# Two step-order tables exchanged in a two-layer graph network on one core

## The chip, the cores and the metric

The kernel runs on one core of one Trainium2 chip. The metric is the device time of one launch in microseconds (us). The kernel before takes 2598.3 us, the median of three runs (2597.79 to 2598.43).

## What is computed

64 graphs of 256 nodes with 512 features, all with one adjacency matrix, pass through two layers. Each layer normalises its input, applies a ReLU, and adds its result to the input. Layer 0 multiplies with the adjacency and then with a weight. Layer 1 is attention with 8 heads of 64 features over the neighbours. Cut to what matters:

```python
h = jnp.maximum(_layernorm(x), 0.0)
x = x + (einsum('nm,bmd->bnd', adj, h) @ w0 + b0)          # layer 0
h = jnp.maximum(_layernorm(x), 0.0)
q, k, v = h @ Wq + bq, h @ Wk + bk, h @ Wv + bv             # layer 1, 8 heads of 64
scores = q @ k.T / 8 + (1 - adj) * -1e9
x = x + softmax(scores) @ v @ Wo + bo
```

All of it is in fp32; a matmul call is two instructions on PE (TensorE).

## The kernel before

**Groups and stages.** Two graphs (GB = 2) make a group of 512 rows; there are NG = 32 groups. Layer 0 runs over all groups first and leaves its results in DRAM (`residual`, `hidden`). Then a loop over g runs layer 1. One turn of it holds, in this order on PE:

- `attend(g, 0)`: the denominators (`pden`, L1248) and softmax times v (`pav`, L1255) for the first half of the heads (qd = 0) of both graphs of the group
- `score(g, 1)`: scores of the second half (`sc`, L1207); DVE (VectorE) adds the mask while it moves each one out of PSUM (L1214)
- **the QK stage**: q and k of group g + 1, in the order of the table `QK` (L1427)
- `attend(g, 1)` and `score(g + 1, 0)`
- **the VO stage**: v of group g + 1 and the output projection of group g, in the order of the table `VO` (L1457)

`QK` is used for g = 1 to 30, 30 times; `VO` for g = 2 to 29, 28 times. Earlier groups use a plainer form, and the last ones the tables `V1`, `O1` and `OL`.

**A projection as steps.** A 512 by 512 product is not done directly. `quartered` (from L589) splits it by Strassen's scheme in Winograd's form into seven half-size products, named A to G; most of these are split the same way once more. It makes a dictionary of small steps, each named by a letter for the matrix (q, k, v, o), a letter for the product, and a letter or digit for the part. `follow` (L836) carries them out in the order of the table: a token is one step, `|` ends a tick, and `x` issues one waiting exponent of the softmax on ACT (ScalarE). So a table fixes the order of instructions on PE, ACT and DVE, and through the ticks also when deferred work on POOL (GpSimd) is issued.

For a product F or G the steps a, c, d and f are matmuls into a small sum bank (`q_Fs`), b, e and g copy intermediate sums from it on ACT, h and l add on DVE, and i, j and k are matmuls into the main bank `pa`. For C, D and E the steps b, e, f and h copy or add the sums into the result in SBUF, and i, j, k and l handle the remaining part. In such a chain a matmul may not start before the copy or addition that reads the sum ahead of it. Steps p and m move a whole main bank into the result or add it there. What `part` and `place` of `quartered` give is a region of the result.

**The steps that the prediction follows.** E of v ends with three steps: `El0` is a copy on ACT, `El1` and `El2` are additions on DVE. They finish the part of v that belongs to the first half of the heads and the second graph:

```python
for name, i, k in (("El1", 0, 0), ("El2", 1, None)):        # L829
    def todo(i=i, k=k):
        o = part(place(0, 1), i, k)
        add(o, part(banks["pa"], i, k), o)
    step(name, todo, "pa")
```

`attend(g, 0)` of the next turn reads v by halves f of 32 columns, then by graph b, then by 128-row tile k, then by four heads, which lie beside each other in PE's columns:

```python
for f in range(2):                                           # L1250
    for b in range(GB):
        v = V[g][qd, b]
        for k in range(NT):
            for h in range(4):
                nc.tensor.matmul(po[f][...], v[:, k, h * HD + f * 32:...], A[h // 2, b][...], ...)
```

**PSUM banks.** There are eight banks. `bank` (L299) takes the first one of the list of free banks that fits, and `give` (L312) appends a bank at the end of the list when its last step has been issued. The list is worked out while the program is built; on the chip the first matmul into a bank waits until the last reader of its former content has finished. So the order of the steps also decides which step waits for which.

**Deferred work.** `after(n, ...)` puts work off by n ticks. On POOL these are the key sums (L1239), the sums of inputs to the smaller products (L516, L619) and part of the softmax's reciprocal (L1272 to L1274). The next h is summed after the last matmul of v has been issued (`multiplied`). SP issues the DMAs: outputs once both halves of a graph are added up, then the next h and the next residual.

Of the kernel before, what the change touches and what calls it, by code (L numbers as in the profile page):

```python
# [73 lines left out]
def general_path(tc, x, adj, w0, b0, wq, bq, wk, bk, wv, bv, wo, bo, out):  # L74
# [137 lines left out]


QK = (
    "qA0 kA0 qFa kA1 qFb x kA2 | qFc kFa qFd kFb kA3 qFe x qCa | qBa kFc kFd qFf kp000 qA1 qFg qA2 kFe | qFh "
    "kp001 qA3 kFf qp000 kCa qBb kFg kCb kFi qBc | kFj kFh qp001 kFk kCc x kFl qBd kCd kCi qCb kCj kCe qBn kCk | "
    "kCf kp100 qCc kCl qFi kp101 qFj qFk qBe x kCg qFl qDa qBf | kGi kCh qBg kGj qp100 kGk qBk qCd qp101 kBa qCe "
    "kBb qCf qBh | kBc qBi qDb kBn qBj qGi qp110 qGj kBd qp111 qGa kBe qGk | qGb qDc qDd qCg qDe qGc qDf qGd kBf "
    "qCh qGe qDi | kBg qDj qDk kBk qGf qm10 qDg qGg qEa kGa qDh qEb kBh | kBi qGh kGb kBj qGl kDa kp110 kGc kGd "
    "kDb kp111 kEa qm11 qEc kGe | qEd kEb kDc qEf kDd kGf qEe kDe kEc kDf kGg kEd qEi qEf2 | kEf kDi kGh kDg kEe "  # L220
    "kGl kDj kDk qEg km11 qEj qEk | qCi kEf2 qEl0 qCj kDh qCk km10 kEi kEj kEk qCl kEg kEl0 | qEh qEl1 kEl1 kEh "
    "qEl2 kEl2 ")
VO = (
    "vA0 oBz vA1 oAz vA2 vA3 x | vCi vFa vCj vCk vFb vBa vp00 vBb vFc x | vFd vCa vCl vFi vFj vFe vFk vCb vBc oA0 "
    "vBn | vFf vCc vFg vGa vCd vBd vFh oA1 x vFl oA2 | vBe vDa vCe vGb oA3 vCf vp10 vBf op00 vGc vBg vGd | vCg "
    "vDb vGe vGi vBk x vGj vCh vGf vDc vDd oFa vGg | vDe vGk vDf oFb vEa vBh vGh vEb vBi vGl vBj oEa vp11 vEc | "
    "oEb vEd oFc vEf vm11 oFd vEe vDi oFe vDg vEf2 vDj vDh vDk | vEi vm10 vEj vEk oGa vEl0 oFf oGb vEg vEl1 oFg "
    "oFi vEl2 | oEc vEh oGc oFj oFh oFk oEd oFl oGd oCa oGe oDa | op10 oB0 oB1 oDb oCb oGf oEe oB2 oEf oGg | oB3 "
    "oGh oGi op11 oGj oGk oCc oGl oCd | oDc oDd oCe oEg om11 oDi oDj oDk oCf oCi oDe | oCj oDf oCk oEi oEh oCg "
    "oCl0 oEj oEk oDg oCl1 | oEl om10 oCh oDh ")  # L230
V1 = (
    "vA0 vFa vA1 vFb vA2 x vFc | vFd vA3 vCa vFe vEa vp00 vGa vFf vEb | vB0 vGb vFg vCb vFi x vGc vFh vGd vFl vCc "
    "vCd vGe | vDa x vCe vB1 vCf vFj vFk vGf vp10 vCg vEc | vCh vEd vGg vB2 vDb x vGh vGi vGj vDc vGl vEf vDd | "
# [1281 lines left out]
```

## Time and profile before

| | |
|---|---|
| median of 3 runs | 2598.3 us |
| profiled execution | 2598.07 us, of which the span is 2596.3 us |
| a QK stage (matmul start to `pden`) | 22.53 us |
| a VO stage | 22.67 us |
| one turn of the loop, QK stage at 1219.50 to the next at 1280.92 | 61.42 us |
| granted PE clock | 1.00 |

In the profile's rows PE is the matmul, PEld the load of its weights, which overlaps it. A row of the timeline gives the start in us, the time from its first start to its last end, engine, source line, operation, tiles out<-in, shape and how many instructions follow one another. All additions of these stages carry the line L850, because a helper issues them; the tile names tell them apart. Matmuls are pipelined, so the row of two 128-wide instructions lasts 0.39 us while the next row begins 0.22 us later: starts have to be compared, not lengths.

### The profile page before, as it was taken

Reading aid. Unit: us, or ns where it says so; the run is one execution under the profiler, and the core shown is the slowest. Engines: PE = TensorE matmul, PEld = TensorE weight load, DVE = VectorE, ACT = ScalarE, POOL = GpSimd, SP = SyncE. Lnnn points to the kernel's source line nnn. Section 1 sums busy time; section 2 is a strip of 40 time slices with the busy share of each in tenths; the row PEclk is TensorE's granted clock in tenths of the full one; section 3 lists DMA queues with packets and bytes.
Section 4 is the critical chain, followed back from the end, with each engine's and each line's share of the span. In section 5 each row is a group of like instructions: output and inputs, shape, how many; then the busy total and the mean of one; then the engine's idle time right before and its main releaser. Section 6 shows DMA issues by size and latency. Waiting matters only on the chain.

```text
span 2596.3 us, 57453 instructions
## 1 busy us (share of the span) xinstructions
PE 2582.3 (99%) x22046; PEld 2306.2 (89%) x22046; DVE 1941.8 (75%) x4284; ACT 1266.9 (49%) x2930; POOL 1834.3 (71%) x2262
## 2 busy tenths in 40 slices
PE   9999999999999999999999999999999999999999
PEld 8999899988888888889888888888888888889887
DVE  6888888885467777777777777777777777777776
ACT  4544444443344545555554545555444545555553
POOL 6788887773687777776666666777777777776664
PEclk9999999999999999999999999999999999999999
DMA  5776666565111222111111111111111222211111
GB/s 148 194 196 182 169 167 181 162 158 135 33 50 50 65 63 63 57 50 50 50 50 50 50 50 50 50 50 50 50 50 51 66 62 62 56 50 50 50 34 51
DMA packets 281111, 211.40 MB, mean 81 GB/s; under 512 B 145920, under 2 KB 212992, under 8 KB 280832
## 3 DMA queue, kind: packets, MB, share of 16 engines
q1 hardware_dynamic: 280224, 206.89, 29.8%
q8 instruction: 176, 2.88, 0.5%
q10 hardware_dynamic: 608, 0.79, 0.1%
q14 instruction: 103, 0.84, 0.1%
HBM read 106.96 MB, written 100.66 MB: 80 GB/s over the span
## 4 chain that ended last, share of the span: by engine, by line
PE 92%; POOL 3%; DVE 2%; ACT 1%; DMA 1%; issue 1%; SPq 0%; DVEq 0%; POOLq 0%; ACTq 0%
PE sc L1207 9%; PE pav L1255 8%; PE pden L1248 2%; PE q_pa L671 2%; PE k_pa L671 2%; PE v_pa L671 2%; PE o_pa L671 2%; PE q_pa L685 2%; PE v_pa L685 2%; PE o_pc L685 2%; PE o_pa L685 2%; PE k_pa L685 2%; PE q_pc L671 2%; PE k_pc L671 2%; PE v_pc L671 1%; PE q_Ds L671 1%
## 5 line engine op out<-in xcount | busy, mean ns | idle before, releaser
L1214 DVE SCALAR_TENSOR_TENSOR a<-sc,maskT 128x512 f32<-128x512 f32 x512 | 312.1, 682 | 237.4 <-PE sc L1207 237.4
L1272 POOL TENSOR_TENSOR as<-as 128x512 f32<-128x512 f32 x64 | 80.7, 1260 | 415.3 <-ACT as L1271 409.1
L1239 POOL TENSOR_TENSOR as<-a 128x512 f32<-128x512 f32 x256 | 318.4, 1274 | 32.9 <-ACT a L1232 27.5
L1232 ACT ACTIVATE a<-a 128x1024 f32<-128x1024 f32 x256 | 271.8, 1062 | 3.6 <-DVE a L1214 3.6
L1255 PE MATMUL pav<-a,v 128*32 128x256 f32 x4096 | 232.7, 379 | 0.0
L1255 PEld LDWEIGHTS pav<-a,v 128*32 128x32 f32 x4096 | 132.9, 110 | 88.1
L43 DVE BATCH_NORM_STATS2 st<-x 128x6 f32<-128x512 f32 x256 | 173.2, 676 | 8.7 <-DMA x<-in_x_dram 6.5
L1262 ACT ACTIVATE as<-pden 128x512 f32<-128x512 f32 x64 | 38.4, 600 | 226.7 <-PE pden L1248 226.7
L1031 ACT ACTIVATE h<-x,nb,rs 128x512 f32<-128x512 f32 x128 | 97.2, 807 | 96.4 <-POOL nb L55 93.9
L1207 PE MATMUL sc<-qk 64*128 64x256 f32 x1024 | 119.2, 382 | 0.0
L1207 PE MATMUL sc<-q,k 64*128 64x256 f32 x1024 | 119.2, 382 | 0.0
L1207 PEld LDWEIGHTS sc<-q,k 64*128 64x128 f32 x1024 | 97.1, 187 | 22.4 <-issue 13.2
L1207 PEld LDWEIGHTS sc<-qk 64*128 64x128 f32 x1024 | 97.1, 187 | 22.3 <-issue 13.1
L708 ACT COPY q_F<-q_Fs 128x128 f32<-128x128 f32 (+1 forms) x90 | 27.1, 301 | 183.2 <-PE q_Fs L671 183.2
L902 ACT ACTIVATE h<-x,nb,rs 128x512 f32<-128x512 f32 x124 | 90.8, 803 | 51.0 <-POOL nb L55 46.6
L965 POOL TENSOR_TENSOR hs<-h 128x512 f32<-128x512 f32 x31 | 39.4, 1271 | 72.9 <-ACT h L902 72.9
L1037 DVE STREAM_TRANSPOSE r<-h 128x512 f32<-128x512 f32 x128 | 84.0, 689 | 6.8 <-ACT h L1031 4.2
L619 POOL TENSOR_TENSOR spare<-h1T,spare 128x128 f32<-128x128 f32 x180 | 82.3, 457 | 7.0
L850 DVE TENSOR_TENSOR x<-o_pa,x 128x512 f32<-128x512 f32 (+1 forms) x121 | 82.8, 685 | 4.5 <-PE o_pa L685 3.1
L516 POOL TENSOR_TENSOR t_y<-yT,t_y 128x512 f32<-128x512 f32 (+1 forms) x65 | 82.7, 1272 | 3.2 <-ACT yT L937 0.8
L1274 POOL TENSOR_TENSOR as<-as 128x512 f32<-128x512 f32 x64 | 80.6, 1259 | 5.4
L309 ACT ACTIVATE o_pc<-bo_r 128x512 f32<-128x512 f32 x30 | 18.0, 601 | 134.6 <-DVE a L1214 134.6
(1659 smaller groups left out, 8882.5 us busy)
## 6 DMA issues: line engine op xcount, KB each, us to landing
residual<-x SPq DMA_DIRECT2D x256, 128.0 KB, 2.6
hidden<-r SPq DMA_DIRECT2D x128, 256.0 KB, 4.4
h1T<-hidden SPq DMA_DIRECT2D x64, 512.0 KB, 7.1
x<-residual SPq DMA_DIRECT2D x32, 1024.0 KB, 8.1
x<-in_x_dram SPq DMA_DIRECT2D x254, 128.0 KB, 3.0
out_dram<-x SPq DMA_DIRECT2D x62, 512.0 KB, 3.6
w_sb<-in_L_gnn_weight_dram SPq DMA_DIRECT2D x1, 1024.0 KB, 9.7
wq_sb<-in_L_gnn_Wq_dram SPq DMA_DIRECT2D x1, 1024.0 KB, 7.2
```

Of the source, the lines that this page charges most:

```text
L43: nc.vector.bn_stats(st, src)
L671: nc.tensor.matmul(o[:, 0, :], lhs, rhs, start=bool(fresh), stop=True, skip_group_check=True)
L685: nc.tensor.matmul(t[:, m, :], lhs, rhs, start=starts, stop=True, skip_group_check=True)
L850: nc.vector.tensor_tensor(o, ps, u, op=ALU.add)
L902: nc.scalar.activation(H0[g][:, t, :], xt[:, t, :], AF.Relu, bias=nb[:, t % n:t % n + 1], scale=rs[:, t % n:t % n + 1])
L1031: nc.scalar.activation(h1[:, k * NT + t, :], xt[:, k * NT + t, :], AF.Relu, bias=nb[:, t:t + 1], scale=rs[:, t:t + 1])
L1037: nc.vector.transpose(r[:, :, k, t, :], h1[:, k * NT + t, :].rearrange("p (j b) -> p j b", b=32))
L1207: nc.tensor.matmul(ps[j][:, kt * N:(kt + 1) * N], k[j * HD:(j + 1) * HD, c, kt * P:(kt + 1) * P], q[j * HD:(j + 1) * HD, c, :], start=(kt ...
L1214: nc.vector.scalar_tensor_tensor(o.rearrange("p k n -> p (k n)"), ps[j], SCALE, maskT_f, op0=ALU.mult, op1=ALU.add)
L1232: nc.scalar.activation(a, a, AF.Exp)
L1239: nc.gpsimd.tensor_tensor(AS[c, b], a4[:, :, 0, :], a4[:, :, 1, :], op=ALU.add)
L1255: nc.tensor.matmul(po[f][h * 32:(h + 1) * 32, b * N:(b + 1) * N], v[:, k, h * HD + f * 32:h * HD + f * 32 + 32], A[h // 2, b][:, (h % 2) * ...
```

## The change

Two constants change: the strings `QK` and `VO`. Each new string holds the same tokens as the old one (190 and 176 with the ticks and the exponents), in another order; steps, shapes and instructions stay as they are. The other tables are the same.

```diff
 QK = (
-    "qA0 kA0 qFa kA1 qFb x kA2 | qFc kFa qFd kFb kA3 qFe x qCa | qBa kFc kFd qFf kp000 qA1 qFg qA2 kFe | qFh "
-    "kp001 qA3 kFf qp000 kCa qBb kFg kCb kFi qBc | kFj kFh qp001 kFk kCc x kFl qBd kCd kCi qCb kCj kCe qBn kCk | "
-    "kCf kp100 qCc kCl qFi kp101 qFj qFk qBe x kCg qFl qDa qBf | kGi kCh qBg kGj qp100 kGk qBk qCd qp101 kBa qCe "
-    "kBb qCf qBh | kBc qBi qDb kBn qBj qGi qp110 qGj kBd qp111 qGa kBe qGk | qGb qDc qDd qCg qDe qGc qDf qGd kBf "
-    "qCh qGe qDi | kBg qDj qDk kBk qGf qm10 qDg qGg qEa kGa qDh qEb kBh | kBi qGh kGb kBj qGl kDa kp110 kGc kGd "
-    "kDb kp111 kEa qm11 qEc kGe | qEd kEb kDc qEf kDd kGf qEe kDe kEc kDf kGg kEd qEi qEf2 | kEf kDi kGh kDg kEe "
-    "kGl kDj kDk qEg km11 qEj qEk | qCi kEf2 qEl0 qCj kDh qCk km10 kEi kEj kEk qCl kEg kEl0 | qEh qEl1 kEl1 kEh "
-    "qEl2 kEl2 ")
+    "kFa kA0 kFb kA1 kFc qFa x qCa | kFd kBa kA2 qFb kA3 kFe x qA0 | kFf qFc qFd kFg qA1 kp000 kFh qA2 kp001 | "
+    "qA3 qFe kFl qBa qp000 qBb qFf qp001 kBb | kFi qFg kFj qCb qBc qFi qFh qBn kFk kBc qCc qFl x qCd kBd qCe kCa "
+    "| qCf qBd kBn qFj kCb kp100 qFk qBe qCg kp101 kBe kCc qCh qp100 kCd qBf | qp101 kCe kBf kCf qDa qBg kGi kBg "
+    "qDb kGj x qBk kGk kBk kCg qGi | kCh qGj qGk qDc qDd qCi qDe qGa qDf qCj | qGb kGa qCk kGb qGc qCl qDg qGd "
+    "kGc qDh qGe kGd | kDa kGe qGf kDb qEa qGg kBh kBi qEb kBj qGh qBh qGl | kp110 qBi qEc kp111 qEd qBj qEe kEa "
+    "kGf qp110 qEf2 kDc | qp111 kDd kDi kEb kDe kDj kDf kGg kDk qDi qEf qm11 qDj qDk | kEc kGh kEd kGl qEi kEe "
+    "qEj qEk kEf km11 kDg qEl0 qEg | kEf2 kCi kDh kCj kCk qEh kEi qEl1 kEj qEl2 kEk kEg kCl kEl0 | qm10 kEh km10 "
+    "kEl1 kEl2 ")
 VO = (
-    "vA0 oBz vA1 oAz vA2 vA3 x | vCi vFa vCj vCk vFb vBa vp00 vBb vFc x | vFd vCa vCl vFi vFj vFe vFk vCb vBc oA0 "
-    "vBn | vFf vCc vFg vGa vCd vBd vFh oA1 x vFl oA2 | vBe vDa vCe vGb oA3 vCf vp10 vBf op00 vGc vBg vGd | vCg "
-    "vDb vGe vGi vBk x vGj vCh vGf vDc vDd oFa vGg | vDe vGk vDf oFb vEa vBh vGh vEb vBi vGl vBj oEa vp11 vEc | "
-    "oEb vEd oFc vEf vm11 oFd vEe vDi oFe vDg vEf2 vDj vDh vDk | vEi vm10 vEj vEk oGa vEl0 oFf oGb vEg vEl1 oFg "
-    "oFi vEl2 | oEc vEh oGc oFj oFh oFk oEd oFl oGd oCa oGe oDa | op10 oB0 oB1 oDb oCb oGf oEe oB2 oEf oGg | oB3 "
-    "oGh oGi op11 oGj oGk oCc oGl oCd | oDc oDd oCe oEg om11 oDi oDj oDk oCf oCi oDe | oCj oDf oCk oEi oEh oCg "
-    "oCl0 oEj oEk oDg oCl1 | oEl om10 oCh oDh ")
+    "vA0 oAz vA1 oBz vA2 vA3 x | vCi vFa vCj vCk vFb vBa vp00 vBb vFc x | vDa vFd vCl vFi vFj vFe vFk vBc oA0 vBn "
+    "| vFf vCa vFg oA1 vCb oA2 vFh x vFl oA3 | vGa op00 vBd vp10 vCc vCd vBe oB0 vGb vDb vCe oFi | vCf vGi vGj x "
+    "vBf vDc vDd vGc vDe vBg vGd | vDf oFj vGe vGk vBk vCg vDg vCh vGf oFa vDh vGg vBh | vEa oFb vBi vGh vEb vBj "
+    "vGl oFc vp11 oFd vEc vEd oFe | vm11 oCa vEe vDi vEf vDj oCb oFf vEf2 vDk oFg oGa vm10 vEi oGb vEj | vEk oFh "
+    "vEg vEl0 oFk oGc vEh oGd oEa oFl oGe oCc | oCd oEb oGf op10 oDa oGg oEc oEd oDb oB1 oGh | oGl oDc oB2 oEe "
+    "oB3 oEf oGi oCe oGj op11 | oEg oGk oCf oDd oCi om11 oCj oCk oCg oDe | oDf oDi oDj oEh oDk oCh oEi oEj om10 "
+    "oEk oDg | oEl oDh oCl0 oCl1 vEl1 vEl2 ")
```

The first two ticks of `VO` hold the same steps as before, but for the places of oAz and oBz. In the old string vEl1 and vEl2 stand in the ninth of fifteen ticks, and the last tick holds oEl, om10, oCh and oDh; in the new one vEl1 and vEl2 are the last two tokens.

## The prediction

> **What bounds the kernel now.** I read the page first, then who waited for whom on PE, then the timeline of single stages.
>
> ```profile
> PE 2582.3 (99%) x22046; PEld 2306.2 (89%) x22046; DVE 1941.8 (75%) x4284; ACT 1266.9 (49%) x2930; POOL 1834.3 (71%) x2262
> ...
> PE 92%; POOL 3%; DVE 2%; ACT 1%; DMA 1%; issue 1%; SPq 0%; DVEq 0%; POOLq 0%; ACTq 0%
> ```
>
> TensorE sets the time: the chain that ended last is PE for 92% of the span. Its listed waits add up to under 8 us, none in a QK or VO stage. But a busy PE is not PE at its peak, so I also compared starts. A 128-wide step of two instructions takes 0.22 us, a 256-wide one 0.43. A QK stage has 84 and 8 of them, 22.21 us; a VO stage 77 and 12, 22.38. The trace shows 22.53 and 22.67, the same in nearly all 58 stages. Of the excess, 0.10 is the first pair behind the scores, 0.09 the change to the denominators, and 0.10 one repeated stall inside:
>
> ```profile
> 1199.17 0.41 DVE L850 TENSOR_TENSOR v_G<-v_Gs,v_G 128x256 f32<-128x256 f32 x1
> ...
> 1199.42 0.39 PE L671 MATMUL v_pc<-wv_sb,spare 128*128 128x128 f32 x2
> 1199.65 0.48 PE L671 MATMUL o_Es<-wo_s,oT 128*128 128x128 f32 x2
> 1199.97 0.28 PE L671 MATMUL v_Es<-spare,spare 128*128 128x128 f32 x1
> ```
>
> o_Es takes 0.32 us to the next start, its neighbours 0.22: vGh, which frees its PSUM bank, ended at 1199.58, 0.07 before it started. The QK twin is q_Ds, whose bank is freed by kCl:
>
> ```profile
> 1228.64 0.39 PE L671 MATMUL k_Cs<-spare,spare 128*128 128x128 f32 x2
> 1228.87 0.49 PE L671 MATMUL q_Ds<-t_h,wq_sb 128*128 128x128 f32 x2
> 1229.20 0.28 PE L671 MATMUL q_Bs<-spare,spare 128*128 128x128 f32 x1
> ```
>
> Following the bank list (give appends, take removes the first that fits) through the old order names exactly these two hand-overs as late. So the rule is: a result that lands 0.18 us or more ahead of its reader costs nothing (vFa behind the seventh score eviction), one that lands 0.06 ahead costs 0.10. DVE and the end of the stage are the place to watch:
>
> ```profile
> 1206.04 0.29 DVE L850 TENSOR_TENSOR x<-o_Ds,x 128x128 f32<-128x128 f32 x1
> ...
> 1211.28 0.69 DVE L850 TENSOR_TENSOR x<-o_pa,x 128x512 f32<-128x512 f32 x1
> 1211.88 0.68 DVE L850 TENSOR_TENSOR x<-o_pc,x 128x512 f32<-128x512 f32 x1
> 1212.48 0.41 DVE L850 TENSOR_TENSOR x<-o_Cs,x 128x256 f32<-128x256 f32 x1
> 1212.81 0.41 DVE L850 TENSOR_TENSOR x<-o_Ds,x 128x256 f32<-128x256 f32 x1
> ```
>
> ```profile
> 1211.39 1.07 PE L1248 MATMUL pden<-as,ones 128*32 128x256 f32 x16
> 1212.28 3.64 PE L1255 MATMUL pav<-a,v 128*32 128x256 f32 x64
> ```
>
> DVE works without a pause from 1206.04 and ends at 1213.22, 1.83 us after the denominators have begun. Today nobody waits for that tail: it holds residual sums, and v was finished at 14.82 us into the stage.
>
> **What the Trainium skill says.** "TensorE: Matmul & The Clock Gate", section "Architectural detail: the array is 16× 32×32, not 1× 128×128": PE may pull a weight load ahead of running matmuls, VectorE and ScalarE are strict first in, first out. The trace agrees: loads of a 128-wide step start 0.11 us ahead of their matmul, and DVE keeps the program's order. Same page, section "The mechanism": matmuls in different column tiles run together. It agrees: 64 pav instructions of 379 ns need 3.46 us, sixteen groups of four at 0.216. "Perfetto Trace Analysis", section "Identifying the Most-Contended Engine", says that matmul busy time is no measure of headroom; here 99% busy hid the 0.10 us stalls.
>
> **The change, part by part.** No instruction is added or removed; QK orders 30 stages, VO 28. Times below are from a stage's first matmul (1219.50 and 1188.72 in the stages read), PE walked at its own pace plus the 0.10 of the first pair.
>
> *Stalls that go.* In the new QK q_Ds takes the bank that qCh frees at 9.76, and reads it at 10.04: no stall. In the new VO o_Es takes the one that oFh frees at 15.27, for 15.83. 30 × 0.10 + 28 × 0.10 = 5.8 us gained, at most, if nothing is late in their place.
>
> *Other hand-overs of the new orders.* I followed each DVE and ACT queue with the spacing of the old rows, and set each end against its reader. Tightest are kBa behind the seventh score eviction (1.86 for a weight load at 1.97), kA0 behind the fourth (0.06 for 0.21), qGc behind the copy qGb (13.18 for 13.27), qFi behind qp001 (6.62 for 6.80) and vEa behind vCh (11.08 for 11.25). With 0.055 us from a DVE end to a weight load (o_Fs behind t_o, 2579.89 to 2579.95) all pass, the closest by 0.03. I take nothing; if one failed it is 0.10 × 30 = 3 us, kept for the range.
>
> *The moved end of VO.* vEl1 and vEl2 go from 14.2 us to the last places of the DVE queue, behind oEl, oDh, oCl0, oCl1. They complete V of head half 0, second batch. The step after the stage is attend(g+1, 0), which reads that part in pav's second quarter of its first half.
>  When DVE is done: oDb starts at 17.14 (oDa at 16.72, second half 0.11 later, DVE 0.31 after that, as in the old rows). From there it has work always: five 512-wide adds at 0.60 = 3.00; seven 256-wide at 0.33 to 0.34 = 2.34; oGh with oGl waiting for its result, 0.46; four 128-wide at about 0.21 = 0.83; two pairs e, f at 0.31 = 0.62; vEl2 itself 0.42. Sum 7.67, so vEl2 ends at 24.81. Check: the old tail took 7.19 (1206.04 to 1213.22); without oCb (0.21), with vEl1 and vEl2 (0.20 and 0.33) and 0.13 for oGl's wait it is 7.64.
>  When PE needs it: without the o_Es stall pden begins at 22.57, pav at 23.46, and after four groups of 0.216 the second batch at 24.32, its second group at 24.54, with weight loads 0.21 ahead. Heads 0 and 1 wait for vEl1 (24.4), heads 2 and 3 for vEl2. Their load can start at 24.81 + 0.055 = 24.87; a restart with 32-wide weights takes 0.24 to the next group (pden: 0.89 for four groups, against 0.864). So that group comes at 25.11 in place of 24.55: **0.56 us in each of 28 stages, 15.7 us**. Behind this wait are the rest of pav, the scores and the next QK stage, all on the bounding engine, so nothing hides it.
>  The trace of before shows no such wait. Bounds: 0.45 (the DVE tail 0.1 shorter) and 0.74 (the load's whole delay counts, as at q_Ds); a gain is excluded, a late reader can't speed PE up. That is 12.6 to 20.7 us.
>
> *What else moves, at nothing.* The fourth exponent of QK starts at 10.4 instead of 8.8 us; its key sum on POOL would have begun at 11.0 and begins at 11.5; the cover is the 10 us to the denominators at 22.5. The last v matmul comes at 14.83 instead of 13.95 and releases POOL's sums of the next h; POOL is busy with key sums until 18.55 there, so they start as before. oAz and oBz change places on an idle ACT. The adds that release the two output DMAs of a stage end at 23.3 and 24.3 (23.25 and 24.5 before); SP then loads h and the residual, which are used a stage or more later. The end of QK on DVE is 24.65 (24.87 before); its readers, the scores, start at 26.98. If that cover went, each 0.1 would be 3 us.
>
> *Sum.* 2598.07 (the profiled execution, 1.8 over its span of 2596.3) − 5.8 + 15.7 = 2608.0; the median of the runs, 2598.3, is 0.2 higher: 2608.2.
>
> **Rivals.** *No wait for v* (ends faster): the DVE tail runs ahead of pav. Then only the two stalls go, 2598.3 − 5.8 = 2592.5. It decides where vEl2 ends before 24.07, the weight load's time less the hand-over: 0.74 earlier than my sum. For it: an order picked for longer copies should have slack in the middle, and it has. Against: DVE's queue there is packed, and the old tail measures the same work at 7.19. *A small wait*: about 0.2 us in place of 0.56, if DVE catches up by half: 28 × 0.2 = 5.6 eats the gain, 2598.1. *The order does what it is named for*: random lateness of evictions is taken up. Only one of 30 QK stages (at 1280.9) is longer, 22.84 against 22.53, so this is 0.3 us in all, and changes no case. *The whole tile v is waited for* before pav's first matmul: (24.87 − 23.46) × 28 = 39 us, about 2632; against it, the copy vp10 into v starts at 7.20 before the add vCf, issued ahead of it into another part of v, ends at 7.78, so parts are tracked apart.
>
> **How the numbers follow.** Wait for v: 0.77, 2608.2, own range 2605 to 2614 (12.6 and 20.7 in the sum give 2605.1 and 2613.2; the rest is for a missed hand-over). No wait: 0.12, 2592.5. Small wait: 0.10, 2598.1, spread over 2594 to 2603.5. Whole tile: 0.01. The range runs from 2596 into the small-wait case up to 2614. About 0.2%, 5.2 us, is what a measurement of this kernel can tell from no change: slower takes the main case and the last one, 0.78; same the small wait, 0.10; faster is the case of no wait, 0.12.
>
> **What would show it.** Right: q_Ds and o_Es at 0.22; VO stages at 22.57 and QK at 22.43; in pav behind VO, and only there, a gap on PE of about half a us that ends with a DVE add into v, so that a pair of stages takes 0.36 more than 61.42. Wrong: vEl2 ending before 24.1, no gap in pav, or new stalls of 0.1 inside a stage, at qGc or kBa first.

## The result and the profile after

The new tables take 2612.4 us (median of 6 runs, 2610.95 to 2612.55) against 2598.3 before: 1.0054 of the time, 95% interval 1.0044 to 1.0064. The kernel became slower by 14.1 us, where 9.9 were forecast.

The first lines of the page after, to be set beside those of before:

```profile
span 2610.4 us, 57427 instructions
## 1 busy us (share of the span) xinstructions
PE 2593.4 (99%) x22046; PEld 2321.3 (89%) x22046; DVE 1941.0 (74%) x4284; ACT 1265.4 (48%) x2930; POOL 1835.2 (70%) x2262
```

Each engine in this row has as many instructions as before (the total differs by 26, in instructions that are not counted as busy), and the busy times of DVE, ACT and POOL are within 2 us of those before. PE is "busy" 11 us longer for the same matmuls, and PEld 15 us longer for the same loads. The page alone says no more. So the time from the first matmul of each part to the first of the next was added up by part, in both traces:

| part | places | before, us | after, us | difference |
|---|---|---|---|---|
| QK stages with the table | 30 | 676.3 (22.53 each) | 672.9 (22.43) | -3.4 |
| VO stages with the table | 28 | 634.9 (22.67) | 636.5 (22.73) | +1.6 |
| pav behind VO | 31, 28 of them after the table | 110.6 (3.57) | 126.5 (4.13 in 28) | +15.9 |
| all else | | | | 0.0 |

The sum is the 14.1 us by which the span grew. Of the two stalls that were to go, q_Ds is free of its own: its row now lasts 0.39 us where it lasted 0.49, as a step without a stall does.

```profile
1233.21 0.39 PE L671 MATMUL q_Ds<-t_h,wq_sb 128*128 128x128 f32 x2
```

These are the first two lines in the list of waits of the weight loads in the new kernel (the columns are total us, times, longest):

```profile
PEld sc L1207 <- issue: 26.3, 64, 0.4
PEld pav L1255 <- DVE v L850: 19.9, 56, 0.5
```

The first line stood there before, with the same numbers. The second did not: twice in each of 28 places (once for vEl1, once for vEl2) a load of pav waits for a DVE addition into v. The same place in the timelines of PEld and DVE:

```profile
1215.16 0.78 PEld L1255 LDWEIGHTS pav<-a,v 128*32 128x32 f32 x16
1216.46 0.14 PEld L1255 LDWEIGHTS pav<-a,v 128*32 128x32 f32 x4 [0.52 <-DVE v L850]
1216.79 2.30 PEld L1255 LDWEIGHTS pav<-a,v 128*32 128x32 f32 x44 [0.19 <-DVE v L850]
```

```profile
1215.60 0.61 DVE L850 TENSOR_TENSOR x<-o_pb,x 128x256 f32<-128x256 f32 x2
1216.12 0.61 DVE L850 TENSOR_TENSOR v<-v_pa,v 128x128 f32<-128x128 f32 x2
```

Sixteen loads, those of the first graph, go through. Then PE stands until vEl1 is done (loads at 1216.46) and again until vEl2 ends at 1216.73 (loads at 1216.79). The stage began at 1191.75, so vEl2 ends 24.98 into it. In the timeline of PE, the matmuls show it only by their length, since they count as one busy row:

```profile
1214.48 1.07 PE L1248 MATMUL pden<-as,ones 128*32 128x256 f32 x16
1215.37 4.20 PE L1255 MATMUL pav<-a,v 128*32 128x256 f32 x64
1219.51 0.70 PE L1207 MATMUL sc<-q,k 64*128 64x256 f32 x4
```

From pav's start to the scores are 4.13 us, against 3.57 before.

A second thing is new: VO stages are not at 22.57, but at 22.73. The stall at the old place is gone, but there is another one, at oEg (PE and DVE of the new kernel):

```profile
1210.66 0.39 PE L671 MATMUL o_pa<-wo_s,t_o 128*128 128x128 f32 x2
1210.88 0.39 PE L671 MATMUL o_pa<-spare,t_o 128*128 128x128 f32 x2
1211.16 0.49 PE L671 MATMUL o_Es<-spare,to 128*128 128x128 f32 x2
1211.49 0.28 PE L671 MATMUL o_pa<-wo_s,to 128*128 128x128 f32 x1
```

```profile
1210.37 0.74 DVE L850 TENSOR_TENSOR x<-o_Es,x 128x128 f32<-128x128 f32 x2
1211.03 0.28 DVE L850 TENSOR_TENSOR x<-o_Cs,x 128x128 f32<-128x128 f32 x1
```

oEg starts 0.28 after its neighbour and takes 0.33, in place of 0.22 twice: 0.16 lost. The first row of DVE holds two additions that read o_Es, oEe and then oEf; oEf ends at 1211.11, 0.05 before oEg starts.

### The profile page after: what moved, and what is told of

Its sections match the earlier page's. It is cut to its first block, busy times and chain, and to the rows that moved or that the text cites. A ratio compares the mean times of both kernels' runs of the same rounds, so it can differ in the third digit from the quotient of the medians.

```text
span 2610.4 us, 57427 instructions
## 1 busy us (share of the span) xinstructions
PE 2593.4 (99%) x22046; PEld 2321.3 (89%) x22046; DVE 1941.0 (74%) x4284; ACT 1265.4 (48%) x2930; POOL 1835.2 (70%) x2262
## 4 chain that ended last, share of the span: by engine, by line
PE 92%; DVE 3%; POOL 2%; DMA 1%; issue 1%; ACT 1%; SPq 0%; DVEq 0%; POOLq 0%; ACTq 0%
PE sc L1207 9%; PE pav L1255 9%; PE q_pa L671 2%; PE k_pa L671 2%; PE v_pa L671 2%; PE pden L1248 2%; PE v_pa L685 2%; PE o_pa L671 2%; PE o_pc L685 2%; PE o_pa L685 2%; PE k_pa L685 2%; PE q_pa L685 2%; PE k_pc L671 2%; PE q_pc L671 2%; PE v_pc L671 1%; PE k_Fs L671 1%
## 5 line engine op out<-in xcount | busy, mean ns | idle before, releaser
L1255 PE MATMUL pav<-a,v 128*32 128x256 f32 x4096 | 247.5, 380 | 1.2
L1255 PEld LDWEIGHTS pav<-a,v 128*32 128x32 f32 x4096 | 155.1, 110 | 81.9 <-DVE v L850 19.9
L708 ACT COPY k_F<-k_Fs 128x128 f32<-128x128 f32 (+1 forms) x90 | 27.2, 302 | 194.2 <-PE k_Fs L671 194.2
L1274 POOL TENSOR_TENSOR as<-as 128x512 f32<-128x512 f32 x64 | 80.7, 1261 | 5.4
L516 POOL TENSOR_TENSOR t_h<-h1T,t_h 128x512 f32<-128x512 f32 x64 | 81.7, 1276 | 2.5
```

The costliest lines, as they stand in the source:

```text
L516: eng.tensor_tensor(self.t[n][:, c, :], self.operand(p, c), self.operand(q, c), op=ALU.subtract)
L1255: nc.tensor.matmul(po[f][h * 32:(h + 1) * 32, b * N:(b + 1) * N], v[:, k, h * HD + f * 32:h * HD + f * 32 + 32], A[h // 2, b][:, (h % 2) * ...
```

## The experiments

Theory: pav waits for the data of vEl2, whose place in DVE's queue is too late. Rivals: the two tables act on each other through the list of banks; the wait belongs to a PSUM bank, or to the end of DVE's queue as a whole. Each ratio is to runs of the kernel before that were made beside the experiment; their median was 2598.2 to 2598.6.

**Each table alone.** `qk_new_vo_old` has the new QK and the old VO, `qk_old_vo_new` the reverse:

```diff
-QK = ("qA0 kA0 qFa ...          # qk_new_vo_old, on the kernel before
+QK = ("kFa kA0 kFb ...
```

> The new QK table with the old VO table. Theory: the loss lies in VO alone, and QK brings 0.10 us in each of 30 stages: QK stages 22.43, VO stages 22.67, softmax times v 3.57 behind both, time about 2595 (3.3 under before). Rival, that the two tables act through the order of the bank list that one stage leaves to the next: then VO stages or the parts behind them change as well, and the time differs from 2595 by more than 2.

> The old QK table with the new VO table. Theory: QK stages 22.53, VO stages 22.73, softmax times v behind VO 4.13 in 28 places, time about 2615.5. Rival (the bank list carries something over): the gap behind VO is another than 0.56, and the time differs from 2615.5 by more than 2.

Measured: 2594.95 (ratio 0.9986, 0.9980 to 0.9993) and 2616.4 (1.0070, 1.0053 to 1.0087). The stages were 22.43, 22.67 and 3.57 in the first, 22.53, 22.73 and 4.13 in the second. The new QK is a gain of 3.6, the new VO a loss of 17.8, together the 14.1 of both tables. So the tables do not act on each other.

**The two additions moved.** In `v_before_oEl` they stand four additions earlier in the queue:

```diff
-    "oEk oDg | oEl oDh oCl0 oCl1 vEl1 vEl2 ")
+    "oEk oDg | vEl1 vEl2 oEl oDh oCl0 oCl1 ")
```

> The new tables, with vEl1 and vEl2 moved ahead of oEl in the last tick of VO; the same work, nothing left out. Theory (pav waits for the data that vEl2 writes): vEl2 ends near 23.5 us into the stage, the gap in pav goes, pav 3.57 everywhere, VO stages stay at 22.73, time 2612.4 - 28 x 0.56 = 2596.7. Rival (pav waits for a PSUM bank that the residual additions oEl, oDh, oCl free, or for the end of DVE's queue as a whole): those end as late as before, the gap stays near 0.56 and the time near 2612.

Measured: 2597.2 us, ratio 0.9994 (0.9986 to 1.0003); VO 22.73, pav 3.57 everywhere. DVE and PE of this kernel:

```profile
1211.33 0.61 DVE L850 TENSOR_TENSOR v<-v_pa,v 128x128 f32<-128x128 f32 x2
1211.86 0.68 DVE L850 TENSOR_TENSOR x<-o_pa,x 128x512 f32<-128x512 f32 x1
1212.46 0.41 DVE L850 TENSOR_TENSOR x<-o_Ds,x 128x256 f32<-128x256 f32 x1
1212.79 0.61 DVE L850 TENSOR_TENSOR x<-o_pb,x 128x256 f32<-128x256 f32 x2
```

```profile
1212.04 3.64 PE L1255 MATMUL pav<-a,v 128*32 128x256 f32 x64
1215.60 1.13 PE L1207 MATMUL sc<-q,k 64*128 64x256 f32 x8
```

vEl2 now ends at 1211.94. DVE's queue is as long as in the new kernel and ends at 1213.40, well after pav has begun, and the additions that free banks end about 0.5 later in the stage than in the new kernel. PE does not wait for them. The rivals of bank and queue fall.

**The reader moved instead.** `pav_by_graph` leaves both tables as they are and exchanges two loops of `attend`:

```diff
-        for f in range(2):
-            for b in range(GB):
-                v = V[g][qd, b]
+        for b in range(GB):
+            v = V[g][qd, b]
+            for f in range(2):
```

> The new tables unchanged, but the loops of softmax times v run over the graph outside and the column half inside, so that the second graph's v is read after eight groups in place of four, 0.86 us later. Theory: vEl2 ends at 24.98, the load that needs it comes at about 25.1 instead of 24.3, so the gap goes: pav 3.57, time about 2596.7 with an unchanged order of additions. Rival (bank or queue): the second half's bank is now wanted 0.86 us earlier, so the gap stays or grows, time 2612 or more.

Measured: 2596.9 us (ratio 0.9995, 0.9986 to 1.0003). DVE of this kernel, whose stage began at 1189.23, and PE:

```profile
1213.60 0.61 DVE L850 TENSOR_TENSOR v<-v_pa,v 128x128 f32<-128x128 f32 x2
```

```profile
1212.85 3.64 PE L1255 MATMUL pav<-a,v 128*32 128x256 f32 x64
1216.41 0.92 PE L1207 MATMUL sc<-q,k 64*128 64x256 f32 x6
```

vEl2 ends at 1214.21, 24.98 into the stage as in the new kernel, and pav takes 3.57 nevertheless. So the time at which the second graph's v is read decides. With the run before, the wait is shown from both sides.

**A smaller dose.** `v_before_one` moves the two additions ahead of oCl1 only:

```diff
-oEl oDh oCl0 oCl1 vEl1 vEl2
+oEl oDh oCl0 vEl1 vEl2 oCl1
```

> The new tables, vEl1 and vEl2 moved ahead of oCl1 alone, so one 128-wide addition of 0.21 us earlier. Theory (the gap follows the end of vEl2 one to one): vEl2 ends 0.21 earlier, the gap is 0.56 - 0.21 = 0.35, pav behind VO 3.92, VO stages 22.73, time 2612.4 - 28 x 0.21 = 2606.5. Rival (bank or end of queue): gap and time as in the new kernel, 0.56 and 2612.4.

Measured: 2606.6 us (ratio 1.0032, 1.0019 to 1.0046), pav behind VO 3.93. The gap is 0.36 for a move of 0.21: one to one.

**The stall inside VO taken away, the late v left.** `oEg_later`:

```diff
-op11 | oEg oGk oCf oDd oCi
+op11 | oGk oCf oDd oEg oCi
```

> The new tables, with the matmul step oEg two steps of PE later in VO (behind oDd), so that it no longer meets the addition oEf; the late vEl1 and vEl2 stay. Theory (behind VO the path goes through DVE's queue, which ends with vEl2 at about 24.98 whatever PE does a little earlier): the stall of 0.16 inside VO goes, VO stages 22.57, but pav's gap grows by as much, to about 0.72, pav 4.29; time unchanged, 2612.4 within 1. Rival (the stall inside VO and the gap in pav add up independently): VO 22.57, pav 4.13, time 2612.4 - 28 x 0.16 = 2607.9.

Measured: 2612.6 us (ratio 1.0055, 1.0040 to 1.0071). VO is 22.57, the stall is gone; pav is 4.29. PE of this kernel:

```profile
1214.70 1.07 PE L1248 MATMUL pden<-as,ones 128*32 128x256 f32 x16
1215.59 1.05 PE L1255 MATMUL pav<-a,v 128*32 128x256 f32 x16
1216.83 3.11 PE L1255 MATMUL pav<-a,v 128*32 128x256 f32 x48 [0.19 <-DVE v L850]
1219.87 0.49 PE L1207 MATMUL sc<-q,k 64*128 64x256 f32 x2
```

What VO wins, the wait takes: 0.16 earlier at pav, 0.16 longer there. Between oDb and vEl2 the path runs through DVE, and this small stall of PE in that stretch costs nothing by itself. The two numbers 0.16 and 0.56 are one delay of 0.72.

**Which reader oEg waits for.** oEe reads the half of bank o_Es that oEg writes, oEf reads the other half. `oEf_later` moves only oEf:

```diff
-oB3 oEf oGi oCe oGj op11 | oEg
+oB3 oGi oCe oGj op11 oEf | oEg
```

> The new tables, with the addition oEf placed behind op11 instead of ahead of oCe. oEf reads the half of bank o_Es that the following step oEg does not write; oEe, which reads the half that oEg writes, stays in its place. Theory (a matmul waits for every reader of its bank, not only of its own half): oEg waits until oEf ends near 20.15, the stall inside VO grows from 0.16 to about 0.9, VO stages near 23.5, time 2618 to 2634. Rival (only the half counts, and 0.16 came from oEe): the stall goes, VO 22.57, and the time stays near 2612.

Measured: 2628.2 us (ratio 1.0114, 1.0099 to 1.0130). VO is 23.51, pav 3.90: together 1.27 lost. PE and DVE of this kernel:

```profile
1214.83 0.39 PE L671 MATMUL o_pa<-spare,t_o 128*128 128x128 f32 x2
1215.89 0.49 PE L671 MATMUL o_Es<-spare,to 128*128 128x128 f32 x2 [0.67 <-DVE x L850]
```

```profile
1214.32 0.28 DVE L850 TENSOR_TENSOR x<-o_Es,x 128x128 f32<-128x128 f32 x1
...
1215.42 0.41 DVE L850 TENSOR_TENSOR x<-o_Es,x 128x256 f32<-128x256 f32 x1
```

oEe is done at 1214.60, but oEg begins only at 1215.89, 0.06 after oEf's end at 1215.83. In this program a matmul waits for all readers of its bank. It guards PSUM by bank, which the Trainium skill ("PSUM — Partial Sum Buffer", section "PSUM bank collisions raise a hardware error") calls the simple version of its rule: to guard by bank and quadrant (32 partitions), not by address. The two halves of o_Es lie in the same 128 partitions, so by that page oEf's read and oEg's matmul may not overlap although the data would allow it; no run here tried it. The price in this run is 0.9 us in each stage. A stall as long as this one also reaches DVE, which stands 0.47 us in the same stage for a matmul of o_pa; so the sum lost is 1.27 and not 0.72.

**Why DVE was later than worked out.** oDb started at 17.35 in place of 17.14. DVE of the new kernel, op10 and oDb:

```profile
1208.32 0.68 DVE L850 TENSOR_TENSOR x<-o_pa,x 128x512 f32<-128x512 f32 x1
1209.10 0.29 DVE L850 TENSOR_TENSOR x<-o_Ds,x 128x128 f32<-128x128 f32 x1
```

`oCe_early` puts an addition into another part of x between op10 and oDb:

```diff
-oGf op10 oDa ... oGi oCe oGj
+oGf op10 oCe oDa ... oGi oGj
```

> The new tables, with the addition oCe moved in VO from behind oEf to directly behind op10. Theory (oDb starts late, at 17.35 instead of the 17.14 of my working, because it adds into the part of x that op10 has just written and waits on DVE for op10 to finish): oCe works on another part and starts at 17.16 in the pause, oDb stays at 17.35, and all behind is 0.20 earlier, vEl2 at 24.78; stall in VO and gap in pav together shrink from 0.72 to 0.52, time 2612.4 - 28 x 0.20 = 2606.8. Rival (op10 keeps DVE busy until 17.35, or oDb waits for PE): oCe starts at 17.35, oDb behind it at 17.55, nothing is gained, time 2612.4.

Measured: 2606.7 us (ratio 1.0032, 1.0020 to 1.0044); VO 22.73, pav 3.94. DVE of this kernel, whose stage began at 1190.51:

```profile
1207.08 0.68 DVE L850 TENSOR_TENSOR x<-o_pa,x 128x512 f32<-128x512 f32 x1
1207.68 0.28 DVE L850 TENSOR_TENSOR x<-o_Cs,x 128x128 f32<-128x128 f32 x1
1207.87 0.28 DVE L850 TENSOR_TENSOR x<-o_Ds,x 128x128 f32<-128x128 f32 x1
```

oCe starts 0.60 behind op10, at 17.17 into the stage; oDb stays at 17.36, 0.11 after op10's end. So in the new kernel DVE was free at 17.17, and oDb waited for something else. That it was PE, this run does not exclude, but the traces do: oDa's second matmul starts 0.52 ahead of oDb in the new kernel and 1.05 ahead in the kernel before (1204.99), and in both oDb starts 0.10 after op10's end. So it waits for op10, which writes the part of x that oDb adds to. Stall and gap together shrank to 0.53, as expected. All of it came out of the gap: the stall at oEg stayed, because only what stood behind oCe's old place came earlier.

**Both corrections**, and the old tables with two steps moved. `both_mended` joins the moves of v_before_oEl and oEg_later. `old_two_moves` is the kernel before with:

```diff
-kCg qFl qDa qBf | kGi kCh
+kCg qFl kGi qDa qBf | kCh
-vBj oEa vp11 vEc |
+vBj vEc vp11 oEa |
```

> The new tables with both corrections: vEl1 and vEl2 ahead of oEl, and oEg behind oDd. Theory: QK 22.43, VO 22.57, pav 3.57 everywhere, time 2598.3 - 30 x 0.10 - 28 x 0.10 - 0.3 = about 2592.3, 0.2% under the kernel before. Rival: another addition becomes late in the packed end of DVE's queue, VO over 22.6, and the time stays at 2594 or more.

> The tables of the kernel before with two matmul steps exchanged in place: kGi ahead of qDa in QK, vEc ahead of oEa in VO, so that both steps come one place later and no longer meet the addition that frees their bank. Theory (the whole good side of the new tables is these two repeated stalls of 0.10): QK 22.43, VO 22.57, pav 3.57, time about 2592.4, as with both tables new and mended. Rival (the new tables are better in other ways too, for instance against irregular lateness): the time stays clearly above 2592.3, and single stages stand out.

Measured: 2592.3 us (ratio 0.9978, 0.9969 to 0.9987) and 2591.9 us (0.9976, 0.9967 to 0.9985). Both have QK at 22.43 (22.42), VO at 22.57, pav at 3.57, and both are faster than the kernel before and the new one. PE of the second, at the place of the old o_Es stall:

```profile
1197.87 0.39 PE L671 MATMUL v_Es<-spare,spare 128*128 128x128 f32 x2
1198.10 0.39 PE L671 MATMUL o_Es<-wo_s,oT 128*128 128x128 f32 x2
1198.32 0.39 PE L671 MATMUL v_Es<-wv_s,h1T 128*128 128x128 f32 x2
```

0.22 from start to start. Two exchanged steps bring as much as the new tables do at their best. A further advantage of the new QK does show, but it is small: in the profiles of the three kernels with the old QK, one or two of 30 QK stages are longer by 0.2 to 0.4 us (before: 22.85; old_two_moves: 22.64; qk_old_vo_new: 22.89 and 22.90), in the nine with the new QK none is by more than 0.02. That is under 1 us of a run, and the two times above do not tell it apart.

## Why the prediction was right, point by point

- **The wait for v**: right in place and cause. It was put in pav's second quarter of the first half, for heads 2 and 3, at 0.56 us in each of 28 stages; pav grew from 3.57 to 4.13. Both moved writers and moved reader show the cause. That the size is hit to 0.01 is in part luck: vEl2 ended 0.17 later than forecast, and pav began 0.16 later, because of the stall at oEg. With VO at the forecast 22.57 the wait is 0.72, as oEg_later shows.
- **The stalls that go**: right for QK, 22.43 as forecast, 3.4 us with the one irregular stage of the run before. For VO the old stall went, but the gain of 2.8 became a loss of 1.6. The failing step is "PE walked at its own pace": the list of tightest hand-overs did not have oEg behind oEf, the last reader of its bank. The omission alone would not have hurt: with oDb at 17.14, as forecast, oEf would end some 0.2 ahead of oEg instead of 0.05, and by the prediction's own rule 0.18 costs nothing. So this stall follows from the next point. This is worked out from the traces; no run has it.
- **When DVE is done**: 24.81 was forecast, 24.98 measured. The mis-sized term is the start of the chain, oDb at 17.14 instead of 17.35: it counts PE's hand-over, and leaves out that oDb adds to what op10 has just written. The rows of before had it: x<-o_Ds at 1206.04 begins 0.10 after x<-o_pa ends at 1205.94, with oDa long done. The other terms of the chain held: from oDb to vEl2's end 7.63 us were measured, 7.67 forecast.
- **The sum**: the two errors are one. The end of pav is set by DVE from oDb on, so 0.17 more on DVE is 0.17 more per stage, whether it shows at oEg or in pav: 28 × 0.17 = 4.8, against 4.2 that the time exceeds the forecast. oEg_later shows it: 0.16 less in VO, and the same time.
- **What else moves, at nothing**: held. Pav behind QK, denominators and scores keep their lengths. One other line is new in the list of the weight loads: the first load of QK, now k_Fs, waits for a POOL row of the softmax's reciprocal (L1274), 0.33 us in 28 places. Before, the first load of QK stood as long at q_pa, with no releaser named, so this costs nothing new.
- **The rivals**: no wait and small wait are excluded by 4.13; the whole-tile wait as well, since the first graph's loads went through. The order as named, against irregular lateness: the prediction put it at 0.3 us in all, and that is its size. The one longer QK stage of before is gone in the new kernel, as in every profile with the new QK, and old_two_moves reaches the time of both_mended without it.

## What to carry to other kernels

A result moved to the end of a queue is only free if its reader is far: follow each moved write to its first reader, beyond the end of the stage that is being ordered, and not to the stage's end. Where the bounding engine is tuned to a few hundredths, work out the chain of the other engine from its own dependences too, an addition onto what the one before it wrote and every reader of a bank included. And before a whole order is replaced, look whether the stalls that it is to remove can be taken away by exchanging two steps.

## What the runs showed of the hardware

- A late hand-over costs PE, in a step of two 128-wide matmuls, about 0.10 us between its two matmuls, besides the delay of its start. It did so where the result landed 0.05 to 0.07 ahead of the first matmul (o_Es before, oEg after), and cost nothing from 0.18 on; what lies between was not measured. In the groups of four 32-wide column tiles a restart costs 0.02: in the new kernel the matmuls that waited for v have 0.24 to the next ones of the same heads, in place of 0.22.
- A DVE addition that does not use what the one in front of it wrote starts 0.08 us before that one's end. One that does starts 0.10 after it (oDb behind op10: 0.79 from start to start behind a 512-wide addition, against 0.60) or 0.03 after it (oEf behind oEe). Both values come back in every stage; what decides between them stays open.
- The order of the profile's rows hides stalls of this size: the 0.10 us lie between the two matmuls of one step, within a row that counts as busy, and no list of waits has them.
